# Layer 0 in passes of one head and 1024 rows, with its values and masks brought back from DRAM, in place of layer 1's sums on Pool and the tensor engine

## The chip, the cores and the metric

The kernel runs on one core of one Trainium2 chip. The metric is the device time of one launch in microseconds, the median of the runs shown. Engines are named as the profile names them: PE is the tensor engine (PEld its weight loads), DVE is Vector, ACT is Scalar, POOL is Pool (GpSimd), and SP is the queue that issues most DMAs.

## The reference, cut to what matters

There are N = 4096 nodes with 512 features. The adjacency matrix `adj` holds zeros and ones, with about one in 128 set. Two layers follow each other.

```python
# layer 0: 4 heads of 128; the logit is a sum of a row term and a column term
support = (x @ weight) per head
logits  = f1[None, :] + f2[:, None];   w = where(logits >= 0, logits, 0.2 * logits)
attn    = softmax(w where adj, else -1e30) * mask
x       = layernorm(x + attn @ support + bias + x @ proj_w + proj_b)
# layer 1: 8 heads of 64; queries, keys and values from x
scores  = q @ k.T * 64 ** -0.5 + 0.01 * eye - 1e16 * (1 - max(adj, eye))
x       = layernorm(x + sum over heads of softmax(scores) @ v @ Wo)
```

Because each logit of layer 0 is a sum of two terms, the kernel doesn't exponentiate a 4096 x 4096 matrix there: the weight is a product of factors per row and per column, and a maximum of two such products. In layer 1 the weights are `exp(q.k)` times the transposed mask, and the division by the sum of weights comes after the product with the values.

## The kernel before, in words

The work is written out by hand in program order (`manual_schedule`). Each engine runs its instructions in that order and waits on semaphores; tile pools with a fixed number of buffers (`bufs`) decide when a tile may be written again. The stages follow one another:

1. **Layer 0, prologue.** For each of eight groups of 512 rows (`g`), PE turns x (L616) and multiplies by `weight` (L628, `s_ps`) and `proj_w` (L632, `b_ps`). Vector makes the row and column terms (L639, L642). Pool adds the biases to x (L622) and scales the values (L594). The values of all heads, with a column of ones times the factor, stay in SBUF in one tile, `sup`. PE also turns the adjacency rows of group 0 (`transpose_adj`, L545), four 128 x 128 blocks per column tile, from four row tiles `arow` of 128 x 4096 that Pool's queue loads (L535).
2. **Layer 0, attention.** The loop runs over `g`, over pairs of heads `b` (two) and over 32 column tiles `j`: 512 steps. Of each step, `front` runs three steps ahead of the products. Scalar makes a step function `z` for each of two heads (L682), Vector takes its minimum with the mask (`az`, L685, 1024 wide) and then makes the weights `p`, one instruction of 512 for each of the two heads (L690). PE multiplies: eight products of a 128 x 128 block of `p` with 129 columns of `sup` (L753). They accumulate in four PSUM banks of two heads each, from six buffers. At the last `j`, `finish` takes the denominators (L703, L705) and divides on Scalar (L707) at once. After the second pair of heads, `close` adds `base` on Pool (L714), normalises on Vector (L504 to L515) and stores, and `turn` transposes for layer 1. While the second pair of heads of a group runs, PE turns the adjacency rows of the next group, in every step.
3. **Layer 1, projections.** Keys, queries and values are made (L794, L801, L810) and stored in DRAM.
4. **Layer 1, attention.** There are 32 pairs (`g`, `m`) of 512 queries and two heads, and 32 units `j` in each. A step takes a batch of three units. PE makes the scores (L883) of the batch, two heads side by side, into PSUM tiles `s_ps` of which there are three. Scalar exponentiates in place (L892). Vector multiplies by the mask into SBUF (`p1`, L898), and frees the PSUM tile. PE then does the products with the values (L918) of the batch before.

The sums of weights in layer 1 go two ways. Of 32 units, 22 are added on Pool (L906, L908, in `q_sum`), and ten (`by_tensor`) are summed on PE with a column of ones (L929). The eleventh batch of a pair has only two units. Its third PSUM tile is used to add up the sums of the pair before (L937, L940) and to project one finished row tile (L967):

```python
            def by_tensor(j):
                return j % 6 in (2, 3) and j < NT - 2
...
                chores.append(extent)
                chores.extend(lambda k=k: invert(k) for k in range(8))
```

`divide` copies the sums on Scalar, and hangs the rest into a list, `chores`: two reductions for the check of the range, eight reciprocals of 64 columns each (L957), and later the layernorm of a row tile, whose last step is on Scalar (L981). One chore is done after each mask product, so that no long piece of work stands in Vector's way.

Of the kernel before, what the change touches and what calls it, by code (L numbers as in the profile page):

```python
# [12 lines left out]
ALU = mybir.AluOpType  # L13
# [416 lines left out]
def tile_gat_then_masked_attention(  # L430
# [27 lines left out]
    QD = P // 4  # L458
    CH = 8
    NCH = NT // CH  # L460

# [16 lines left out]
    least = const.tile([P, NG * NP1], F32, name="least")  # L478
    total = const.tile([P, NG * NP1], F32, name="total")
    pick = const.tile([P, HP, KD], F32, name="pick")  # L480
    nc.gpsimd.memset(pick, 0.0)
    for e in range(HP):
        for n in range(2):
            r = (n * HP + e) * QD
            nc.gpsimd.memset(pick[r:r + 1, e, :], 1.0)
# [3 lines left out]
    fr_d = [dram.tile([2, H0, G], F32, name=f"fr_d{g}") for g in range(NG)]  # L489
    adjT_d = [dram.tile([P, NT, G], BF16, name=f"adjT_d{g}") for g in range(NG)]  # L490
# [11 lines left out]
    def moments(y):  # L502
        st = small.tile([P, 6], F32, name="bn_st")
        nc.vector.bn_stats(st, y)  # L504
        mv = small.tile([P, 2], F32, name="bn_mv")
        nc.vector.bn_aggr(mv, st)
        ve = small.tile([P, 1], F32, name="bn_ve")
        nc.gpsimd.tensor_scalar(ve, mv[:, 1:2], EPS, None, op0=ALU.add)
        rs = small.tile([P, 1], F32, name="bn_rs")
        nc.gpsimd.tensor_tensor(rs, ve, minus_half, op=ALU.pow)  # L510
        return mv, rs

    def layernorm(dst, y):
        mv, rs = moments(y)
        nc.vector.tensor_scalar(dst, y, mv[:, 0:1], rs, op0=ALU.subtract, op1=ALU.mult)  # L515
# [3 lines left out]
    W0 = D0 + 1  # L519
    with tc.tile_pool(name="l0", bufs=1) as l0, \  # L520
            tc.tile_pool(name="l0a", bufs=GT) as arow_p, \
            tc.tile_pool(name="l0t", bufs=NCH + 1) as adjT_p:
        sup = l0.tile([P, NT, H0, W0], F32, name="sup")
# [4 lines left out]
        arow = {}  # L528
        adjT = {}

        def load_rows(g):
            arow[g] = []
            for t in range(GT):
                a = arow_p.tile([P, N], BF16, name="arow")
                nc.gpsimd.dma_start(a, adj[(g * GT + t) * P:(g * GT + t + 1) * P, :])  # L535
                arow[g].append(a)

        def transpose_adj(g, j, ps):


            if j % CH == 0:
                adjT[g, j // CH] = adjT_p.tile([P, CH, G], BF16, name="adjT")
            p = ps.tile([P, GT, P], BF16, name="at_ps", bufs=1)
            for t in range(GT):
                nc.tensor.transpose(p[:, t, :], arow[g][t][:, j * P:(j + 1) * P], ident_b)  # L545

            def go():
                dst = adjT[g, j // CH]
                nc.scalar.activation(dst[:, j % CH, :], p.rearrange("p t r -> p (t r)"), AF.Copy)  # L549
                if j % CH == CH - 1:  # L550
                    nc.sync.dma_start(adjT_d[g][:, j - CH + 1:j + 1, :], dst)
                if j == NT - 1:
                    del arow[g]
            return go

        with tc.tile_pool(name="l0s", bufs=2) as sp, \
# [19 lines left out]
            load_rows(0)  # L576
            nc.vector.tensor_add(bb[:, 0, :], bb[:, 0, :], bb[:, 1, :])

            def factors(g):
# [12 lines left out]
                for t in range(GT):  # L592
                    i = t0 + t
                    nc.gpsimd.tensor_tensor(sup[:, i, :, 0:D0], sup[:, i, :, 0:D0],  # L594
                                            a[:, t, :, None].to_broadcast([P, H0, D0]),
                                            op=ALU.mult)
                    nc.gpsimd.tensor_copy(sup[:, i, :, D0], a[:, t, :])

                def rest():
# [3 lines left out]
                    nc.vector.tensor_copy(row, p)  # L603
                    nc.sync.dma_start(
                        fr_d[g].rearrange("k h (t r) -> (k h t) r", r=P), row)
                later.at(3, rest)

            for g in range(NG):
# [12 lines left out]
                for t in range(GT):  # L621
                    nc.gpsimd.tensor_tensor(xg[:, t, :], xg[:, t, :], bb[:, 0, :], op=ALU.add)  # L622
                for t in range(GT):
# [11 lines left out]
                    nc.scalar.activation(sup[:, i, :, 0:D0],  # L635
                                         s_ps.rearrange("p (h d) -> p h d", h=H0), AF.Copy)
                    for k, f in ((0, f1[:, i, :]), (1, f2[:, i, :])):
                        prod = sp.tile([P, H0, D0], F32, name="prod", bufs=1)
                        nc.vector.tensor_tensor(prod, sup[:, i, :, 0:D0],  # L639
# [7 lines left out]
                factors(g)  # L647
# [8 lines left out]
        with tc.tile_pool(name="l0w", bufs=2) as wp, \  # L656
# [3 lines left out]
            HG = 2  # L660
            fr_t, bases, aggs, o_t, p_t = {}, {}, {}, {}, {}

            def load_fr(g, b):
                fr_t[g, b] = wp.tile([P, 2, HG, G], F32, name="fr_t")
                src = fr_d[g]
                nc.sync.dma_start(
                    fr_t[g, b].rearrange("p k h r -> p k (h r)"),
                    bass.AP(tensor=src.tensor, offset=src.offset + b * HG * G,
                            ap=[[0, P], [H0 * G, 2], [1, HG * G]]))

            def front(g, b, j):
                if g == 0 and b == 0 and j == 0:
                    load_fr(g, b)
                if j == 4:
                    if b + 1 < H0 // HG:
                        load_fr(g, b + 1)
                    elif g + 1 < NG:
                        load_fr(g + 1, 0)
                fr = fr_t[g, b]
                z = wp.tile([P, HG, G], BF16, name="z")  # L680
                for e in range(HG):
                    nc.scalar.activation(z[:, e, :], fr[:, 0, e, :], AF.Abs,  # L682
                                         bias=f1s[:, j, b * HG + e:b * HG + e + 1], scale=BIG)
                az = wp.tile([P, HG, G], BF16, name="az")
                nc.vector.tensor_tensor(  # L685
                    az, adjT[g, j // CH][:, j % CH, None, :].to_broadcast([P, HG, G]), z,
                    op=ALU.min)
                p = wp.tile([P, HG, G], F32, name="p", bufs=LA + 1)
                for e in range(HG):
                    nc.vector.scalar_tensor_tensor(  # L690
                        p[:, e, :], fr[:, 1, e, :], dj[:, j, b * HG + e:b * HG + e + 1],
                        az[:, e, :], op0=ALU.max, op1=ALU.mult)
                p_t[g, b, j] = p
                if j == NT - 1:
                    del fr_t[g, b]

            def finish(g, b, o):
                for t in range(GT):
                    i = g * GT + t
                    if b == 0:  # L700
                        aggs[i] = wp.tile([P, H0, D0], F32, name="agg", bufs=GT + 1)
                    den = small.tile([P, HG], F32, name="den")
                    nc.vector.tensor_scalar(den, o[t][:, :, D0], 1e-30, None, op0=ALU.max)  # L703
                    rinv = small.tile([P, HG], F32, name="rinv")
                    nc.vector.reciprocal(rinv, den)  # L705
                    for e in range(HG):
                        nc.scalar.activation(aggs[i][:, b * HG + e, :], o[t][:, e, 0:D0], AF.Copy,  # L707
                                             scale=rinv[:, e:e + 1])
                    if b == H0 // HG - 1:
                        later.at(2 + t, lambda i=i, t=t: close(i, t, g))  # L710

            def close(i, t, g):
                y = aggs.pop(i).rearrange("p h d -> p (h d)")
# [3 lines left out]
                later.at(3, lambda: turn(y, t, g))  # L717

            def turn(y, t, g):
# [3 lines left out]
                later.at(1, lambda: turned(p, t, g))  # L723

            def turned(p, t, g):
                x1T = wp.tile([P, KC, P], F32, name="x1T")
                nc.scalar.activation(x1T, p, AF.Copy)
                nc.sync.dma_start(x1T_d[g][:, :, t * P:(t + 1) * P], x1T)

            steps = [(g, b, j) for g in range(NG) for b in range(H0 // HG) for j in range(NT)]  # L730
            for n in range(LA):
                front(*steps[n])
            for n, (g, b, j) in enumerate(steps):
                if n + LA < len(steps):
                    front(*steps[n + LA])
                if j == 0:
                    o_t[g, b] = [ps.tile([P, HG, W0], F32, name="o_ps", bufs=6)
                                 for _ in range(GT)]
                    if b == 0 and g + 1 < NG:
                        load_rows(g + 1)  # L740
                if j == NT // 2 and b == H0 // HG - 1:
                    for t in range(GT):
                        i = g * GT + t
                        bases[i] = wp.tile([P, D], F32, name="base1", bufs=GT + 1)
                        nc.sync.dma_start(bases[i], base_d[i])
                take = None
                if b == H0 // HG - 1 and g + 1 < NG:
                    take = transpose_adj(g + 1, j, ps)
                o = o_t[g, b]
                p = p_t.pop((g, b, j))  # L750
                for e in range(HG):
                    for t in range(GT):
# [334 lines left out]
```

## Time and profile before

| What | us |
|---|---|
| time, median of 3 runs | 4323.43 (4320.09 to 4325.5) |
| the profiled execution: its time | 4323.43 |
| the profiled execution: span | 4321.6 |
| start to the first product of layer 0 (L753) | 305.6 |
| layer-0 attention, to the last L753 | 305.6 to 1536.1 |
| tail, to the first projection of layer 1 (L794) | to 1568.4 |
| projections, to the first scores (L883) | to 1910.7 |
| layer-1 attention, to the last product (L918) | 1910.7 to 4280.8 |
| end | to 4321.6 |

The engines' busy times over the span: PE 3973.1, DVE 2670.6, ACT 1983.9, POOL 1833.1 us. A busy time is a union: two matmuls that run side by side in different rows or columns of the array count once, so count times mean duration is more than the busy time. Every float32 matmul shows as two instructions. DMA moved 371.76 MB, 86 GB/s on average.

In an answer of the timeline, a line gives the start, the time from there to the end of the merged instructions, the engine, the line of the kernel, the operation and the count, and in brackets how long the engine had been idle and what released it.

### The profile page before, as it was taken

To read this page: it belongs to the slowest core of one execution; us is meant where nothing else is said; L and a number is where in the kernel's file an instruction comes from. 1 tells how busy PE (TensorE), PEld (TensorE's weight loads), DVE (VectorE), ACT (ScalarE), POOL (GpSimd) and SP (SyncE) were. 2 spreads that over 40 slices of the span, in tenths; PEclk is the share of its full clock that TensorE was granted. 3 is DMA by queue.
4 is the path that set the end of the run, shared out by engine and by line. 5 is a ranking of instruction groups with operands and counts; after the bars stand their busy time and mean duration, and the time that the engine had idled before them with its cause. 6 is when DMAs were issued, how large, how long until landed. Compare 5 with 4: busy or idle time off the path is not lost.

```text
span 4321.6 us, 53623 instructions
## 1 busy us (share of the span) xinstructions
PE 3973.1 (92%) x20746; PEld 2040.6 (47%) x20746; DVE 2670.6 (62%) x3488; ACT 1983.9 (46%) x2721; POOL 1833.1 (42%) x1083
## 2 busy tenths in 40 slices
PE   6989889889888879989999999999999999999997
PEld 3448789788888844433323323233222323233232
DVE  3559889888888930125665555655555565555554
ACT  1227677667667610024444444444444444444443
POOL 2220000000000010027777667676767667676765
PEclk8999999999999989999999999999999999999999
DMA  4231341342232032332222222222222223222211
GB/s 136 74 113 45 93 118 50 91 116 73 75 108 74 26 117 97 107 142 75 103 75 71 105 76 78 95 78 76 98 71 100 84 67 111 67 80 93 78 61 43
DMA packets 143674, 371.76 MB, mean 86 GB/s; under 512 B 20016, under 2 KB 53040, under 8 KB 129072
## 3 DMA queue, kind: packets, MB, share of 16 engines
q1 hardware_dynamic: 126848, 318.94, 21.3%
q0 software_dynamic: 6080, 42.99, 4.5%
q10 hardware_dynamic: 10480, 6.29, 0.5%
q8 instruction: 165, 2.70, 0.3%
q14 instruction: 101, 0.83, 0.1%
HBM read 305.14 MB, written 92.41 MB: 92 GB/s over the span
## 4 chain that ended last, share of the span: by engine, by line
PE 51%; DVE 7%; POOL 3%; ACT 2%; DMA 2%; issue 1%; SPq 0%; DVEq 0%; POOLq 0%; ACTq 0%
PE s_ps L883 18%; PE o_ps L918 18%; DVE p L898 4%; PE sm_ps L929 4%; PE k_ps L794 3%; PE v_ps L810 3%; PE q_ps L801 3%; PE s_ps L967 2%; ACT s_ps L892 2%; POOL q_sum L908 2%; DVE p L690 1%; DMA md<-adjT_d 1%; PE s_ps L937 1%; ACT y L981 1%; DVE bn_st L504 0%
## 5 line engine op out<-in xcount | busy, mean ns | idle before, releaser
L908 POOL TENSOR_TENSOR q_sum<-q_sum,p 128x1024 f32<-128x1024 f32 x640 | 1506.7, 2354 | 436.0 <-DVE p L898 398.4
L898 DVE TENSOR_TENSOR p<-s_ps,adjT 128x1024 f32<-128x1024 f32 x896 | 1053.0, 1209 | 737.5 <-ACT s_ps L892 723.8
L892 ACT ACTIVATE s_ps<-s_ps 128x1024 f32<-128x1024 f32 x1024 | 981.1, 1008 | 982.1 <-PE s_ps L883 972.2
L753 PE MATMUL o_ps<-sup,p 128*128 128x129 f32 x8192 | 1055.8, 287 | 92.2 <-DVE rinv L705 54.0
L883 PE MATMUL s_ps<-q_sb,k_sb 64*128 64x512 f32 x4096 | 1034.3, 629 | 103.2 <-DVE p L898 90.0
L753 PEld LDWEIGHTS o_ps<-sup,p 128*128 128x128 f32 x8192 | 995.9, 200 | 119.7 <-ACT agg L707 68.5
L918 PE MATMUL o_ps<-p,v_sb 128*64 128x512 f32 x4096 | 973.3, 610 | 0.0
L682 ACT ACTIVATE z<-fr_t,f1s 128x512 bf16<-128x512 f32 x1024 | 680.4, 718 | 285.9 <-DVE az L685 271.2
L690 DVE SCALAR_TENSOR_TENSOR p<-fr_t,dj,az 128x512 f32<-128x512 f32 x1024 | 724.0, 748 | 54.3 <-PE o_ps L753 1.1
L883 PEld LDWEIGHTS s_ps<-q_sb,k_sb 64*128 64x128 f32 x4096 | 362.7, 189 | 754.7 <-DVE p L898 359.0
L918 PEld LDWEIGHTS o_ps<-p,v_sb 128*64 128x64 f32 x4096 | 267.5, 139 | 681.6 <-issue 652.0
L685 DVE TENSOR_TENSOR az<-adjT,z 128x1024 bf16<-128x1024 bf16 x512 | 350.6, 685 | 54.6 <-ACT z L682 54.6
L535 POOL DMA_DIRECT2D arow<-in_adj_dram x32 | 18.0, 578 | 789.1 <-PE at_ps L545 789.0
L549 ACT ACTIVATE adjT<-at_ps 128x512 bf16<-128x512 bf16 x256 | 153.0, 598 | 147.2 <-PE at_ps L545 146.1
L898 DVE TENSOR_TENSOR p<-s_ps,md 128x1024 f32<-128x1024 f32 x128 | 151.6, 1210 | 105.1 <-ACT s_ps L892 96.8
L906 POOL TENSOR_TENSOR q_sum<-p,p 128x1024 f32<-128x1024 f32 x32 | 75.1, 2345 | 255.0 <-DVE p L898 255.0
L929 PE MATMUL sm_ps<-p,ones 128*32 128x512 f32 x1280 | 170.5, 605 | 0.0
L714 POOL TENSOR_TENSOR agg<-agg,base 128x512 f32<-128x512 f32 x32 | 40.4, 1261 | 279.9 <-ACT agg L707 277.1
L838 POOL DMA_DIRECT2D md<-adjT_d x8 | 5.0, 625 | 352.6 <-DMA v_d<-vg 352.6
L797 DVE COPY kg<-k_ps 128x512 f32<-128x512 f32 x32 | 22.1, 691 | 191.4 <-PE k_ps L794 185.2
L957 DVE RECIPROCAL r<-den 128x64 f32<-128x64 f32 x256 | 136.9, 539 | 0.0
L794 PE MATMUL k_ps<-xT,wk 128*128 128x512 f32 x256 | 117.5, 602 | 11.2 <-DMA xT<-x1T_d 11.2
(89 smaller groups left out, 1972.6 us busy)
## 6 DMA issues: line engine op xcount, KB each, us to landing
k_sb<-k_d SPq DMA_DIRECT2D x128, 512.0 KB, 3.5
v_sb<-v_d SPq DMA_DIRECT2D x128, 512.0 KB, 3.5
arow<-in_adj_dram POOLq DMA_DIRECT2D x32, 1024.0 KB, 18.7
adjT_d<-adjT SPq DMA_DIRECT2D x32, 1024.0 KB, 4.1
adjT<-adjT_d SPq DMA_DIRECT2D x32, 1024.0 KB, 5.7
fr_t<-fr_d SPq DMA_DIRECT2D x16, 1024.0 KB, 8.3
x_sb<-in_x_dram SPq DMA_DIRECT2D x8, 1024.0 KB, 5.6
base_d<-base SPq DMA_DIRECT2D x32, 256.0 KB, 2.0
```

What stands on the lines that cost most here:

```text
L549: nc.scalar.activation(dst[:, j % CH, :], p.rearrange("p t r -> p (t r)"), AF.Copy)
L682: nc.scalar.activation(z[:, e, :], fr[:, 0, e, :], AF.Abs, bias=f1s[:, j, b * HG + e:b * HG + e + 1], scale=BIG)
L685: nc.vector.tensor_tensor(az, adjT[g, j // CH][:, j % CH, None, :].to_broadcast([P, HG, G]), z, op=ALU.min)
L690: nc.vector.scalar_tensor_tensor(p[:, e, :], fr[:, 1, e, :], dj[:, j, b * HG + e:b * HG + e + 1], az[:, e, :], op0=ALU.max, op1=ALU.mult)
L753: nc.tensor.matmul(o[t][:, e, :], p[:, e, t * P:(t + 1) * P], sup[:, j, b * HG + e, :], start=(j == 0 and e == 0), stop=(j == NT - 1), ski ...
L794: nc.tensor.matmul(k_ps, w3["wk"][:, c, m * P:(m + 1) * P], xT[:, c, :], start=(c == 0), stop=(c == KC - 1))
L883: nc.tensor.matmul(s[:, e, :], k[r, a:a + P], qt[g, m][r, :], start=True, stop=True)
L892: nc.scalar.activation(s, s, AF.Exp)
L898: nc.vector.tensor_tensor(p, s, mask.to_broadcast([P, HP, G]), op=ALU.mult)
L908: nc.gpsimd.tensor_tensor(q_sum[g, m], q_sum[g, m], p, op=ALU.add)
L918: nc.tensor.matmul(o[r, :], v[:, j % CH, r], p[:, e, :], start=(j == 0), stop=(j == NT - 1))
L929: nc.tensor.matmul(sm_t[g, m][r:r + QD, :], ones[:, 0:QD], pt[g, m, j - 1 + n][:, e, :], start=(j == 3), stop=(j + 6 >= NT - 2))
```

## The change

It has two parts that share no code. **In layer 0** a pass is one head and 1024 rows (`W`), 16 passes of 32 steps as before. One instruction of 1024 makes `z`, and one makes `p`. `sup` is no longer kept: the prologue writes it to DRAM by head (`sup_d`), and each pass loads its head (`sup_t`, 2.1 MB). The transposed masks are no longer kept either: PE turns eight blocks at a time, Scalar copies them into a small `stage`, and they go to DRAM and come back one pass ahead (`load_adjT0`). Adjacency rows come in pieces of 1024 x 512 with two buffers. The prologue turns 1024 rows in place of 512; in the attention a turn comes every third step of the first 96 of 128 steps. The eight row tiles of a pass take three PSUM banks of six, so a new pass has three free banks; the divisions are spread over the eight steps after the pass, and the closes over every second step.

**In layer 1** the sums on PE, `pick`, `chores` and the batch of two units go. Of 32 units, every third is added on Vector (`qs_d`, in SBUF) and the others on Pool (`qs_p`). Six units after the end of a pair, an item "sum" takes one of the three places of a batch: Vector adds both sums, PE adds over partitions, and Vector does a reciprocal of 512, the product, and two instructions for the check of the range. Two items "y" per group each project two row tiles (in one PSUM tile) and normalise them, on Vector alone but for two small Pool instructions.

```diff
+    W = 1024
@@ layer 0, prologue
+                for h in range(H0):
+                    nc.sync.dma_start(sup_d[h][:, t0:t1, :], sup[:, :, h, :])
+                    if i % CJ == CJ - 1:
+                        load_adjT0(0, i // CJ)
@@ layer 0, front
-                for e in range(HG):
-                    nc.vector.scalar_tensor_tensor(
-                        p[:, e, :], fr[:, 1, e, :], dj[:, j, b * HG + e:b * HG + e + 1],
-                        az[:, e, :], op0=ALU.max, op1=ALU.mult)
+                if j == 2 * LA and n + 1 < len(passes):
+                    load_pass(*passes[n + 1])
+                if h == H0 - 1 and w + 1 < NW and j % CJ == 2:
+                    load_adjT0(w + 1, j // CJ)
+                nc.vector.scalar_tensor_tensor(p, fr[:, 1, :], dj[:, j, h:h + 1], az,
+                                               op0=ALU.max, op1=ALU.mult)
@@ layer 0, end of a pass
+                for t in range(WT):
+                    later.at(1 + t, lambda t=t: divide(t))
+                if h == H0 - 1:
+                    for t in range(WT):
+                        later.at(1 + t, lambda t=t: load_base(w, t))
+                        later.at(4 + 2 * t, lambda t=t: close(w, t))
@@ layer 0, steps
-                if b == H0 // HG - 1 and g + 1 < NG:
-                    take = transpose_adj(g + 1, j, ps)
+                if w + 1 < NW and u % 3 == 0 and u // 3 < NT:
+                    take = transpose_adj(w + 1, u // 3, ps)
@@ layer 1, weigh
-                if by_tensor(j) or j == 0:
-                    return
+                if j % 3 == 2:
+                    if j == 2:
+                        qs_d[g, m] = wp.tile([P, HP, G], F32, name="qs_d")
+                        nc.vector.tensor_copy(qs_d[g, m], p)
+                    else:
+                        nc.vector.tensor_tensor(qs_d[g, m], qs_d[g, m], p, op=ALU.add)
@@ layer 1, the sum of a pair
+            def sum_rows(g, m):
+                q = qs_p.pop((g, m))
+                nc.vector.tensor_tensor(q, q, qs_d.pop((g, m)), op=ALU.add)
...
             def divide(g, m, s):
+                nc.vector.reciprocal(r, s[:, 0, :])
+                nc.vector.tensor_tensor(on_t[g][:, m, :], o_t.pop((g, m)), r, op=ALU.mult)
+                nc.vector.scalar_tensor_tensor(fine, s[:, 0, :], SUM_MIN, fine, op0=ALU.is_ge,
+                                               op1=ALU.mult)
+                nc.vector.scalar_tensor_tensor(fine, s[:, 0, :], SUM_MAX, fine, op0=ALU.is_le,
+                                               op1=ALU.mult)
@@ layer 1, batches
+            for batch in batches:
+                got = [fronts[it[0]](*it[1:]) for it in batch]
+                for it, s in zip(batch, got):
+                    mids[it[0]](*it[1:], s)
+                for it in last:
+                    if it[0] == "unit":
+                        products(*it[1:])
```

In the last fence `fronts` of an item are its scores (`scores`, `sum_rows`, `project`) and `mids` what follows on the other engines (`weigh`, `divide`, `close1`).

## The prediction

> **What bounds the kernel now.** I read the page's engine totals first, then the busy time by stage, then the timeline of one quiet stretch in each attention.
>
> ```profile
> PE 3973.1 (92%) x20746; PEld 2040.6 (47%) x20746; DVE 2670.6 (62%) x3488; ACT 1983.9 (46%) x2721; POOL 1833.1 (42%) x1083
> ```
> ```profile
> 305.00:1536.00 1231.00, 1089.90 (x9199) 1053.06 (x9200) 1103.56 (x1741) 831.73 (x1393) 70.22 (x108) 0.94 0.27 79
> ...
> 2300.00:2700.00 400.00, 384.71 (x1670) 120.07 (x1668) 230.90 (x241) 177.03 (x192) 280.01 (x140) 0.98 0.24 83
> ```
>
> The columns are the stretch, its length, then PE, PEld, DVE, ACT, POOL busy. PE's 92% is two different things. In layer 0 PE and Vector are equally full; in layer 1 PE has 96% and Vector 58%.
>
> ```profile
> 402.46 1.86 PEld L753 LDWEIGHTS o_ps<-sup,p 128*128 128x128 f32 x16
> ...
> 403.26 0.68 DVE L685 TENSOR_TENSOR az<-adjT,z 128x1024 bf16<-128x1024 bf16 x1
> 404.05 1.41 DVE L690 SCALAR_TENSOR_TENSOR p<-fr_t,dj,az 128x512 f32<-128x512 f32 x2
> 404.25 0.32 PEld L545 LDWEIGHTS <-arow 128*128 128x128 bf16 x4
> ...
> 404.52 1.86 PEld L753 LDWEIGHTS o_ps<-sup,p 128*128 128x128 f32 x16
> ```
>
> In layer 0 Vector repeats every 2.12 us (the next `az` is at 405.38). PE's 16 loads take 1.86, with four turns 2.07. So **Vector sets the pace of a step**. The timeline of the pass ends (L703) gives passes of 71.2 us and, where four closes follow, 83.1: a close costs 3.0. Check: 512 x 2.12 = 1085, 28 closes = 84, 16 pass ends at (71.2 - 32 x 2.12) = 3.4 make 54; sum 1223 against 1230 measured. The 3.4 are this:
>
> ```profile
> 378.34 2.17 ACT L707 ACTIVATE agg<-o_ps,rinv 128x128 f32<-128x128 f32 x8 [4.74 <-DVE den L703]
> ...
> 379.01 2.74 PEld L753 LDWEIGHTS o_ps<-sup,p 128*128 128x128 f32 x12 [5.37 <-ACT agg L707]
> ```
>
> A new pass needs four PSUM banks and two are free, so PE waits for the divisions, and Scalar's divisions hold up the next `z`.
>
> ```profile
> 2681.93 2.79 PE L918 MATMUL o_ps<-p,v_sb 128*64 128x512 f32 x12
> ...
> 2684.66 1.07 PE L929 MATMUL sm_ps<-p,ones 128*32 128x512 f32 x8
> ...
> 2685.65 2.85 PE L883 MATMUL s_ps<-q_sb,k_sb 64*128 64x512 f32 x12
> ...
> 2687.94 3.49 DVE L898 TENSOR_TENSOR p<-s_ps,adjT 128x1024 f32<-128x1024 f32 x3 [3.08 <-ACT s_ps L892]
> ...
> 2690.44 9.65 POOL L908 TENSOR_TENSOR q_sum<-q_sum,p 128x1024 f32<-128x1024 f32 x4 [2.36 <-DVE p L898]
> ```
>
> In layer 1 **PE sets the pace**: a batch of three units takes 5.51 us, 6.49 with sums on PE. Vector needs 1.16 for a mask product, Pool 2.41 for an add. A pair takes 74 us.
>
> **What the Trainium skill says.** "SBUF — State Buffer", section "Who interferes with whom": a Vector instruction with two SBUF inputs (or in a two-port mode) and a Pool instruction that reads SBUF exclude each other for a whole instruction. L898 reads PSUM and one SBUF operand, so before it doesn't meet this; the new add of `qs_d` does. The trace agrees in the prologue: `prod` takes 0.69 us alone, and
>
> ```profile
> 72.08 5.38 POOL L622 TENSOR_TENSOR x_sb<-x_sb,bb 128x512 f32<-128x512 f32 x4
> ...
> 75.44 0.89 DVE L639 TENSOR_TENSOR prod<-sup,uv 128x512 f32<-128x512 f32 x1 [3.65 <-ACT sup L635]
> ```
>
> 0.89 beside Pool, whose longest L622 is 1.72 in place of 1.26. L515 has 0.55 alone and 1.48 while L714 runs. Also, Vector gets in between two Pool adds that stand ready. "TensorE: Matmul & The Clock Gate", Part 1: PE falls to half its clock after some idle us. The trace agrees: 16 products take 3.29 us after the wait above, else 2.00.
>
> **Layer 0, part by part.** *Steps.* One `p` instruction of 1024 replaces two of 512. What 512 more elements cost I take from L898 (1209 ns for 1024) and L644 (689 for 512): 0.52. Two starts were 0.705 apart, so a step costs Vector 2.12 - 0.705 + 0.52 = 1.935. Scalar's `z`, by the same kind of slope (L892 1008, L947 597 ns), is 0.72 + 0.41 = 1.13, with a mask copy of 1.0 every third step: 1.5, beside Vector. PE: 1.86, and 0.42 more in every third step that turns eight blocks: 2.00. So PE becomes the bound where it turns, Vector elsewhere.
> Row blocks: w = 0: 96 x 2.00 + 32 x 1.935 = 254. w = 1, 2: 19 steps with eight closes, 19 x 1.935 + 24 = 61, then 77 x 2.00 and 32 x 1.935: 277 each. w = 3: 61 + 109 x 1.935 = 272. Sum 1080. Pass ends: three banks are free, PE waits for nothing; Vector's small ones, 3 x 0.27 a pass, are 13. A slow PE clock after the closes: 10, my choice, 0 to 25. Total 1103 for 1230: **-127**.
> *Prologue.* PE turns 128 blocks more, 32 x 0.26 = +8 (a step is 7.14 us, of which the 16 matmuls are 6.87). The first `bb` landed at 36.3 behind 8 MB of rows; now 2 MB stand before it: of 13 MB 7 are left, 36 x 7/13 = 20: -16. `sup_d` stores wait for Pool in SP's queue, ahead of `base_d` and the next x; x has a group (31 us) of time. The first pass needs its stores landed and 2.1 MB loaded, beside `fr_t` (10.4 us before, when 8 MB of rows shared the queues): +6, bounds 0 and 15. Sum **-2**.
> *Reloads.* 16 `sup_t` and 32 masks add 76 MB to 372; the stage then moves about 190 GB/s, where the first slice of the page shows 136 at 0.4 of the DMA engines. They come a pass ahead: nothing, unless late (below). On Pool's queue a row load waits for PE's turns of the load before last, with the next close's add queued behind it; those turns lie three steps back, and PE is past them. On SP a mask load waits for the mask's last reader with nothing urgent behind it. Layer 1 reads the masks in rows of 1 KB rather than 8, a pair ahead: nothing; `md`, for which Vector waits, 0 to 3 us each, 0 taken.
> *Tail.* Eight closes of 3.3 in place of four, but `x1T` is stored as they go, not after them: **+7**.
>
> **Layer 1, part by part.** *PE's work.* Units stay at 1024 x 1.837 = 1881. Gone: sums 160 x 0.98 = 157; L937 and L940 31 x 1.87 = 58 become 31 x 0.93 = 29; projections stay at 102. PE's work falls from 2198 to 2012, **-186**. Before, 2370 were measured: 172 idle.
> *The new adds.* 9 of 1.2 us a pair (L577, two SBUF inputs, 0.69 for 512; 0.52 for 512 more), a copy (0.6 to 1.2) and the merge 1.2. In a quiet batch Vector has 3 x 1.16 + 1.2 = 4.7 of 5.51; but two Pool adds and one Vector add exclude each other, 4.82 + 1.2 = 6.0. The mask products have 1.6 us before PE needs their PSUM tile (2684.86 for the third, against 2679.15 + 5.51 + 1.85). At 0.5 a batch, with a Pool idle at the start of each stretch, this lasts about 6 of 10 batches: 1 us a pair, **31**.
> *The sum item.* Merge, reciprocal 3.3 (L957: 64 columns 0.43 from start to start), product 0.69, checks 1.4: Vector has 1.2 + 5.4 that stand between mask products, and the item holds one of three PSUM tiles until the checks are done. Worked from the batch start at 0 with the sum in third place: Vector free at 2.8, merge to 4.0, PE's sum waits from 1.85; mask products to 6.35, an add waiting for Pool 7.6, the chain to 13.0; PE, at 9.6, wants that tile for the third scores and waits 3.4. PE loses 2.2 + 3.4 = 5.6; in first place 6.9, in second 6.7. A slow clock adds 1 to 2: 8.3 x 31 = **257**. Bounds: 5 (no lock), 12 (Pool first at every tie).
> *The y items.* Vector waits for two small Pool instructions behind Pool's adds, about 13 us for two tiles; PE's project of 7.3 and scores cover it: 1 x 14. `load_md` (57 us of Vector's idle time before, the wait for `md` and the loads in front) stays, 60.
> Sum: 2012 + 31 + 257 + 14 + 60 = 2374: **+4**. The end, without nine chores in a row: **-3**.
>
> **Total.** -2 - 127 + 7 + 4 - 3 = -121, from 4321.6: 4200.6; 1.8 lie outside the span, and this execution is the median run: **4202**.
>
> **The rivals.**
> *A. The lock costs little.* For: Pool has slack, 52 of 74 us. Against: L639 and L515. The event is 5 and quiet batches 5.51: -31 x 4.3 = -133: 4070.
> *B. Slower: Pool holds the port.* If Pool's waiting add goes first each time, merge and adds each wait 2.4 more: event 12, and quiet batches go at 6.0 rather than 5.51 in 8 of 11, +4 a pair: 31 x (3.7 + 3) = +208: 4410. It decides from a pair of 78 us on: the 121 over 31 is 3.9 a pair. For: a queued Pool add stands ready at nearly each tie. Against: `prod` waited 0.2 us, not a whole add.
> *C. Layer 0 waits for rows.* A 2 MB load has 12 steps, 24 us. Four together now land in a median of 18.7, but in pieces of 16 KB rather than 2. At 30 us it costs 21 x 6 = 126: 4328, no change.
>
> **Numbers.** As worked 0.56 (own range 4120 to 4290), A 0.12, B 0.20, C 0.08, smaller slips 0.04. Under 4090 half of A, above 4400 half of B: 4090 to 4400. A measurement tells 0.2%, 9 us, from no change. Faster 0.70, same 0.06, slower 0.24.
>
> **What would show it.** Layer 0: `p` at 1.27 us, steps of 1.94 and 2.00, no wait of PE on `agg`, 1103 from first to last product. Layer 1: adds on Vector with means over 1.2 and Pool's above 2354 ns; PE idle 5 to 7 us at each sum item, released by Vector's checks; pairs of 74. Wrong, if pairs take over 78, if PE's turns wait for `arow`, or if the layer-0 stage stays above 1200.

## The result and the profile after

The changed kernel takes **4395.13 us** (median of 4 runs, 4381.29 to 4405.39); the kernel before took 4323.35 (4 runs, 4320.09 to 4325.5) beside it. The ratio is **1.0165, 95% interval 1.0136 to 1.0194**: slower by 1.65%, which is clear of the noise, though less than 2%. The forecast was 4202 and faster. The profiled execution is the slowest of the four, 4405.39 with a span of 4403.5, so its stages lie about 10 us above those of the median run in sum.

Stages of both traces, cut at the first and last start of the products that bound them (us):

| | before | after | change | predicted |
|---|---|---|---|---|
| start to first layer-0 product | 305.6 | 314.0 | +8.4 | -2 |
| layer-0 attention, first to last product | 1230.5 | 1178.7 | -51.8 | -127 |
| closes, to the first keys | 32.3 | 41.1 | +8.8 | +7 |
| projections, to the first scores | 342.3 | 342.9 | +0.6 | 0 |
| layer-1 attention, to the last product | 2370.1 | 2490.2 | +120.1 | +4 |
| end | 40.8 | 36.6 | -4.2 | -3 |
| sum | 4321.6 | 4403.5 | +81.9 | -121 |

Two stages are off: layer 0 gained 75 us less than predicted, and layer 1 was put 116 too low. First the engine totals of the page and the stretches that answer to those shown of before (columns: stretch, length, then PE, PEld, DVE, ACT, POOL busy, PE clock, DMA share, GB/s).

```profile
PE 3851.6 (87%) x19338; PEld 1999.3 (45%) x19338; DVE 3364.9 (76%) x3134; ACT 1795.0 (41%) x1953; POOL 2014.4 (46%) x1014
```
```profile
314.00:1493.00 1179.00, 1063.91 (x9048) 1020.52 (x9048) 1032.16 (x1187) 699.83 (x752) 68.62 (x95) 0.97 0.41 120
2300.00:2700.00 400.00, 338.71 (x1330) 105.45 (x1328) 336.31 (x256) 155.99 (x161) 276.43 (x119) 0.94 0.23 75
```

In layer 1 PE fell from 96% to 85%, and Vector rose from 58% to 84%, though PE's work was cut. No engine is full there any more, so what layer 1 lost must be in waits.

**Layer 0**, Vector's timeline around the end of a pass late in the stage, where PE turns nothing:

```profile
1424.10 1.28 DVE L695 SCALAR_TENSOR_TENSOR p<-fr_t,dj,az 128x1024 f32<-128x1024 f32 x1
1425.30 0.68 DVE L693 TENSOR_TENSOR az<-adjT,z 128x1024 bf16<-128x1024 bf16 x1
1426.09 1.28 DVE L695 SCALAR_TENSOR_TENSOR p<-fr_t,dj,az 128x1024 f32<-128x1024 f32 x1
1427.29 0.15 DVE L710 TENSOR_SCALAR den<-o_ps 128x3 f32<-128x3 f32 x1
1427.48 0.18 DVE L713 RECIPROCAL rinv<-den 128x3 f32<-128x3 f32 x1
1429.19 0.69 DVE L693 TENSOR_TENSOR az<-adjT,z 128x1024 bf16<-128x1024 bf16 x1 [1.53 <-ACT z L691]
```

and Scalar's timeline in the same place:

```profile
1422.06 1.15 ACT L691 ACTIVATE z<-fr_t,f1s 128x1024 bf16<-128x1024 f32 x1 [0.84 <-DVE az L693]
1427.75 0.37 ACT L714 ACTIVATE agg<-o_ps,rinv 128x128 f32<-128x128 f32 x1 [4.54 <-DVE rinv L713]
1428.02 1.14 ACT L691 ACTIVATE z<-fr_t,f1s 128x1024 bf16<-128x1024 f32 x1
```

A step is 1.99 us (1424.10 to 1426.09). At the end of a pass, Scalar's next `z` stands behind `agg`, which waits for `rinv`, which stands on Vector behind `p`. Scalar idles 4.54 us. In every step it waits 0.84 for a free `z` buffer; in the other 3.70 it could have made the next `z`. Then Vector idles 1.53 for that `z`. This comes three times a pass, once for each bank.

**Layer 1**: the two groups of adds on the page (busy us, then mean ns).

```profile
L934 POOL TENSOR_TENSOR qs_p<-qs_p,p 128x1024 f32<-128x1024 f32 x672 | 1772.4, 2637 | 566.9 <-DVE p L921 525.7
```
```profile
L928 DVE TENSOR_TENSOR qs_d<-qs_d,p 128x1024 f32<-128x1024 f32 x288 | 589.0, 2045 | 9.9
```

The shortest `qs_d` takes 1.22 us, so 0.82 of each on average is waiting; Pool's mean was 2354 before. A quiet stretch (no y item, no mask load), Vector, then PE; the views end inside the last group of each:

```profile
2604.73 1.29 DVE L928 TENSOR_TENSOR qs_d<-qs_d,p 128x1024 f32<-128x1024 f32 x1
2605.94 2.34 DVE L921 TENSOR_TENSOR p<-s_ps,adjT 128x1024 f32<-128x1024 f32 x2
2609.69 1.22 DVE L921 TENSOR_TENSOR p<-s_ps,adjT 128x1024 f32<-128x1024 f32 x1 [1.41 <-ACT s_ps L915]
2610.95 3.23 DVE L928 TENSOR_TENSOR qs_d<-qs_d,p 128x1024 f32<-128x1024 f32 x1
2614.10 2.34 DVE L921 TENSOR_TENSOR p<-s_ps,adjT 128x1024 f32<-128x1024 f32 x2
```
```profile
2612.90 1.13 PE L910 MATMUL s_ps<-q_sb,k_sb 64*128 64x512 f32 x4
2615.37 1.83 PE L910 MATMUL s_ps<-q_sb,k_sb 64*128 64x512 f32 x6 [1.33 <-DVE p L921]
```

Here the add stands behind the *first* mask product of its batch (1.22, then 3.23, then two products). PE makes one score tile (x4) and waits for the other two, whose buffers the two late products free. The pattern repeats every 12.88 us (PE's wait at 2602.49, 2615.37, 2628.26): 6.44 a batch instead of 5.51. In another group of queries, the same kernel:

```profile
2053.41 3.49 DVE L921 TENSOR_TENSOR p<-s_ps,adjT 128x1024 f32<-128x1024 f32 x3 [0.30 <-ACT s_ps L915]
2056.94 1.91 DVE L928 TENSOR_TENSOR qs_d<-qs_d,p 128x1024 f32<-128x1024 f32 x1
2058.91 3.49 DVE L921 TENSOR_TENSOR p<-s_ps,adjT 128x1024 f32<-128x1024 f32 x3
2062.44 2.14 DVE L928 TENSOR_TENSOR qs_d<-qs_d,p 128x1024 f32<-128x1024 f32 x1
```

The add stands *third*, behind all three products. It waits too, and batches go at 5.5. Units with `j % 3 == 2` don't keep their place: 32 units and a sum item are 33, which keeps it within a group of queries, and the two y items shift it by one from group to group. From first write to first write of `qs_d`, a pair without y items takes 68.6 us where the add is third (groups 0, 3, 6; mean of 10), 74.1 where it is second (groups 1, 4, 7; 8 pairs), 74.1 where it is first (groups 2, 5; 6 pairs). The sum item moves along: it is third, second and first in the same groups. The seven pairs with the y items, six of which also load the next mask, take 98.2.

### The profile page after: what moved, and what is told of

It is laid out like the page before. It is cut to its first block, busy times and chain, and to the rows that moved or that the text cites. A ratio compares the mean times of both kernels' runs of the same rounds, so it can differ in the third digit from the quotient of the medians.

```text
span 4403.5 us, 49845 instructions
## 1 busy us (share of the span) xinstructions
PE 3851.6 (87%) x19338; PEld 1999.3 (45%) x19338; DVE 3364.9 (76%) x3134; ACT 1795.0 (41%) x1953; POOL 2014.4 (46%) x1014
## 4 chain that ended last, share of the span: by engine, by line
PE 41%; DVE 15%; issue 5%; POOL 3%; ACT 2%; DMA 2%; DVEq 0%; SPq 0%; ACTq 0%; POOLq 0%
PE s_ps L910 15%; PE o_ps L944 14%; DVE p L921 8%; DVE qs_d L928 3%; POOL qs_p L934 3%; PE s_ps L973 3%; PE k_ps L804 3%; PE v_ps L820 2%; PE q_ps L811 2%; ACT s_ps L915 2%; DVE qs_p L949 2%; PE s_ps L953 1%; DMA md<-adjT_d 1%; PE o_ps L763 1%; DVE bn_st L505 0%
## 5 line engine op out<-in xcount | busy, mean ns | idle before, releaser
L934 POOL TENSOR_TENSOR qs_p<-qs_p,p 128x1024 f32<-128x1024 f32 x672 | 1772.4, 2637 | 566.9 <-DVE p L921 525.7
L910 PE MATMUL s_ps<-q_sb,k_sb 64*128 64x512 f32 x4096 | 1073.2, 644 | 218.6 <-DVE p L921 162.6
L763 PE MATMUL o_ps<-sup_t,p 128*128 128x129 f32 x8192 | 1020.7, 284 | 107.0 <-DVE p L695 77.3
L763 PEld LDWEIGHTS o_ps<-sup_t,p 128*128 128x128 f32 x8192 | 970.4, 196 | 145.3 <-DVE p L695 89.4
L691 ACT ACTIVATE z<-fr_t,f1s 128x1024 bf16<-128x1024 f32 x512 | 585.0, 1148 | 293.5 <-DVE az L693 266.9
L695 DVE SCALAR_TENSOR_TENSOR p<-fr_t,dj,az 128x1024 f32<-128x1024 f32 x512 | 657.6, 1284 | 54.8 <-DVE az L693 1.8
L928 DVE TENSOR_TENSOR qs_d<-qs_d,p 128x1024 f32<-128x1024 f32 x288 | 589.0, 2045 | 9.9
L549 ACT ACTIVATE stage<-at_ps 128x1024 bf16<-128x1024 bf16 x128 | 129.7, 1013 | 113.3 <-PE at_ps L542 110.0
L953 PE MATMUL s_ps<-qs_p,ones 128*64 128x512 f32 x128 | 55.5, 953 | 109.9 <-DVE qs_p L949 109.9
L645 DVE TENSOR_TENSOR prod<-sup,uv 128x512 f32<-128x512 f32 x64 | 51.3, 801 | 118.5 <-ACT sup L641 118.5
## 6 DMA issues: line engine op xcount, KB each, us to landing
arow<-in_adj_dram POOLq DMA_DIRECT2D x32, 1024.0 KB, 11.1
```

The source lines that it names most:

```text
L691: nc.scalar.activation(z, fr[:, 0, :], AF.Abs, bias=f1s[:, j, h:h + 1], scale=BIG)
L695: nc.vector.scalar_tensor_tensor(p, fr[:, 1, :], dj[:, j, h:h + 1], az, op0=ALU.max, op1=ALU.mult)
L763: nc.tensor.matmul(o[t // BK][:, t % BK, :], p[:, t * P:(t + 1) * P], sup_t[w, h][:, j, :], start=(j == 0 and t % BK == 0), stop=(j == NT ...
L910: nc.tensor.matmul(s[:, e, :], k[r, a:a + P], qt[g, m][r, :], start=True, stop=True)
L928: nc.vector.tensor_tensor(qs_d[g, m], qs_d[g, m], p, op=ALU.add)
L934: nc.gpsimd.tensor_tensor(qs_p[g, m], qs_p[g, m], p, op=ALU.add)
```

## The experiments

Ratios are to the kernel before, run beside them, at 4322.0 to 4323.2 us.

**e1_order.** Is the lost layer-0 gain the order on Scalar's queue?

```diff
-                    later.at(1 + t, lambda t=t: divide(t))
+                    if t % BK == 0:
+                        later.at(1 + t, lambda t=t: invert(t // BK))
+                    later.at(2 + t, lambda t=t: divide(t))
```

(`invert` is the part on Vector, `divide` what is left on Scalar.)

> Layer 0: Scalar's divisions are issued one step after Vector's reciprocals instead of in the same step; nothing else moves. Theory (order of the queues): at each of the 48 bank closes of layer 0 the division stands in Scalar's queue ahead of the next z and waits for a reciprocal that stands in Vector's queue behind p, so Vector waits about 1.55 us for z. With the edit z goes first and the waits vanish: layer-0 attention from 1179 to 1105 us, whole 4395 - 75 = 4320. Rival (Scalar or PE is simply short of time when a pass ends, or rows and banks are late): the waits stay, 1165 to 1179, whole 4380 to 4395.

4316.7 us, ratio 0.9985 (0.9965 to 1.0004): 78 less than the changed kernel. Layer-0 attention goes from 1178.7 to 1111.8, which is 67. The other 11 can't be told from noise: layer 1, whose code is the same, took 2470.4 in this trace and 2490.2 in the other, and executions of the changed kernel alone lie between 4381 and 4405. Vector's timeline:

```profile
1364.67 0.15 DVE L708 TENSOR_SCALAR den<-o_ps 128x3 f32<-128x3 f32 x1
1364.86 0.18 DVE L711 RECIPROCAL rinv<-den 128x3 f32<-128x3 f32 x1
1364.95 0.66 DVE L693 TENSOR_TENSOR az<-adjT,z 128x1024 bf16<-128x1024 bf16 x1
```

`az` follows at once; two ends of banks lie 6.23 us apart in place of 7.87. The order was the cause.

**e2_third and e2_first.** Does the place of the add decide, or does an add cost the same wherever it stands, because Pool holds the shared SBUF port?

```diff
-                if j % 3 == 2:
-                    if j == 2:
+                if n == 2:                  # e2_first: n == 0; n is the place in the batch
+                    if (g, m) not in qs_d:
```

> Layer 1: Vector's share of the sums is taken from the unit that stands third in its batch, in place of the unit with j % 3 == 2, whose place in the batch moves with the sum and y items. Theory (place): a Vector add behind the third mask product delays nobody, one in front of a mask product delays PE's score tiles. Pairs go at 69 us in all groups, the layer-1 stage from 2490 to about 2380, whole 4395 - 110 = 4285. Rival (Pool holds the shared port at every tie, rival B of the prediction): the place doesn't matter, the count of adds is about the same, whole 4375 to 4415.

> The opposite of the run above: Vector's share is always the unit that stands first in its batch. Theory (place): all pairs go as in the groups that have it in first place now, 72 to 75.7 us; the nine pairs that take 69 lose about 5 each, whole 4395 + 45 = 4440 (4410 to 4460). Rival (Pool holds the port wherever the add stands): 4375 to 4415.

Third: 4270.0 us, 0.9875 (0.9859 to 0.9892); a quiet pair takes 67.8 on average of 24. First: 4465.0, 1.0323 (1.0306 to 1.034); 74.9. Now compare the adds themselves, the group of e2_third and then that of e2_first:

```profile
L928 DVE TENSOR_TENSOR qs_d<-qs_d,p 128x1024 f32<-128x1024 f32 x308 | 627.6, 2038 | 10.6
```
```profile
L928 DVE TENSOR_TENSOR qs_d<-qs_d,p 128x1024 f32<-128x1024 f32 x311 | 647.3, 2081 | 10.7
```

Nearly the same number of adds, waiting 0.8 to 0.9 us each, and the two kernels are 195 us apart. **Not how long the add waits, but who stands behind it on its queue.** In third place, three products and an add take 5.73 us (in e2_third 2507.27 to 2513.01), so Vector is still a little over PE's 5.51.

**e3_one_input.** Is it the exclusion, or would 1.2 us of Vector in that place cost as much? The add becomes a reduction of the same tile with one input; this kernel leaves the weights of those units out of the sums.

```diff
-                        nc.vector.tensor_tensor(qs_d[g, m], qs_d[g, m], p, op=ALU.add)
+                        nc.vector.tensor_reduce(one, p.rearrange("p e r -> p (e r)"), AX.X, ALU.add)
```

> Each Vector add of layer 1 is replaced, in its old place, by a reduction of the same tile with one SBUF input and 1024 elements, about as long; the weights of those units (j % 3 == 2 but j = 2) are left out of the sums. The merge and everything else stay. Theory (the add costs because it and Pool's adds exclude each other): the reductions take 1.0 to 1.3 us without waiting, Pool's adds fall back to 2.36 us but for the merge, batches go at 5.51 wherever the unit stands, pairs at 67 to 69, whole 4395 - 110 = 4285. Rival (Vector's time in front of the mask products is enough by itself, lock or no lock): batches stay at 6.4 in the groups with the unit first or second, whole 4375 to 4400.

4229.0 us, 0.9782 (0.9766 to 0.9799); a quiet pair takes 66.7 on average, 66.2 to 67.0 by the place. The reductions (min, median, max ns):

```profile
L929 DVE TENSOR_REDUCE one<-p x288: 1219/1220/1222, 1888.9 to 4188.5; 128x1 f32<-128x1024 f32 x144
```

As long as an add alone, in the old places, and not one waited; Pool's mean fell to 2389 ns. So the loss needs both: the exclusion, and a bad place (66.7 without the one, 67.8 without the other, 74.9 with both in e2_first). The Trainium skill, "SBUF — State Buffer", section "Who interferes with whom", says that a Vector reduction on this chip never meets Pool at the shared ports, and an add of two SBUF inputs does; both groups agree.

**e4_l1_before, e5_order_l1_before.** Do the stages add up? Layer 0 of the changed kernel, or that of e1_order, with the old layer 1.

```diff
+            def of_group(g, j0, j1):
+                r = g * G % W
+                return adjT_d[g * G // W][:, j0:j1, r:r + G]
-                nc.sync.dma_start(at[g, c], adjT_d[g][:, c * CH:(c + 1) * CH, :])
+                nc.sync.dma_start(at[g, c], of_group(g, c * CH, (c + 1) * CH))
```

> The prologue and layer 0 of the changed kernel with the layer 1 of the kernel before (sums on Pool and PE); masks are read from the new layout. Theory (layer 1's loss comes from Vector's adds and the sum item, and the stages add up): the layer-1 stage is 2370 us as before, the earlier stages keep what the changed kernel gains, 35 us: whole 4323 - 35 = 4288. Rival (the masks' new layout in DRAM, pieces of 1 KB, or the shift of what stands before it, slows layer 1): the stage stays near 2490 and the whole near 4395.

> The run above with Scalar's divisions one step after the reciprocals in layer 0. Theory: the 67 to 78 us of e1_order come again, 4288 - 72 = 4216. Rival (a faster layer 0 only moves a wait to the tail or to layer 1's first loads): 4270 to 4288.

4289.5 us, 0.9926 (0.991 to 0.9943), and 4222.5, 0.9768 (0.9752 to 0.9784). In e4 layer 1 runs from 1872.9 to 4242.5, 2369.6 us in place of 2370.1. The new layout of the masks costs nothing; all of layer 1's loss is in the sums and items.

**e6_pe_merge.** What makes the sum item cost 8 us? This is one in the changed kernel, on Vector and then on PE:

```profile
2657.36 1.65 DVE L928 TENSOR_TENSOR qs_d<-qs_d,p 128x1024 f32<-128x1024 f32 x1
2658.94 3.35 DVE L949 TENSOR_TENSOR qs_p<-qs_p,qs_d 128x1024 f32<-128x1024 f32 x1
2664.45 3.36 DVE L960 RECIPROCAL r<-s_ps 128x512 f32<-128x512 f32 x1 [2.16 <-PE s_ps L953]
```
```profile
2654.33 2.79 PE L944 MATMUL o_ps<-p,v_sb 128*64 128x512 f32 x12
2662.44 1.97 PE L953 MATMUL s_ps<-qs_p,ones 128*64 128x512 f32 x4 [5.31 <-DVE qs_p L949]
2664.34 3.79 PE L910 MATMUL s_ps<-q_sb,k_sb 64*128 64x512 f32 x8
```

The merge takes 3.35 instead of 1.21, since it meets an add of the next pair on Pool. PE waits 5.31, and then goes at about half clock: 1.97 and 3.79 for what takes 1.08 and 1.99 in e6_pe_merge. Together 8.0. This item stands first in its batch. PE's wait for the merge is 5.3 there on average, 3.5 where the item is second and 2.1 where it is third. The Trainium skill, "TensorE: Matmul & The Clock Gate", Part 1, says that idle time halves PE's clock; this agrees here (1.97 to 1.08, 3.79 to 1.99).

```diff
-                nc.vector.tensor_tensor(q, q, qs_d.pop((g, m)), op=ALU.add)
+                for n, q in enumerate((qs_d.pop((g, m)), qs_p.pop((g, m)))):
...
+                                         start=(n == 0), stop=(n == 1))
```

> e2_third with the merge of the two sums left to PE: four products into the same PSUM rows in place of Vector's add and two products (four of 0.23 us more for each pair). Theory (at each sum item PE waits for the merge, which waits for a Pool add of the next pair, and PE's clock is low afterwards): PE's wait of 5 us and most of the slow 3 us go, a pair from 67.5 to about 63, whole 4270 - 31 x 4.5 = 4130. Rival (the chain of reciprocal, product and checks on Vector sets the item, as the prediction worked it): PE waits a little later instead, only the merge's own 1.2 us go, 4230 to 4240.

4178.4 us, 0.967 (0.9654 to 0.9686): 92 below e2_third, between the two theories. A quiet pair falls from 67.8 to 65.0. The wait for the merge is gone, and a shorter one comes later, on PE:

```profile
2598.04 2.80 PE L944 MATMUL o_ps<-p,v_sb 128*64 128x512 f32 x12
2603.21 4.55 PE L910 MATMUL s_ps<-q_sb,k_sb 64*128 64x512 f32 x12 [2.38 <-issue]
```

The profile names no releaser for it, but Vector's chain from the reciprocal to the second check runs from 2597.72 to 2603.11 there, and PE goes on as it ends. So both were in the item: the merge ahead, Vector's chain behind. With the merge goes a difference between groups. In e2_third, where the add is third everywhere, a pair still takes 65.7, 68.0 and 71.0 us with the sum item third, second and first; here it takes 65.3, 64.1 and 65.9.

**e7_all, e8_max_last, e9_diag_pool.** e6 with the order of e1; and `load_md` no longer makes Vector stand at the landing (in e2_third `md` was waited for 8.60 us at 2538.88, PE 9.11). Where the diagonal is set differs:

```diff
+                if m == 2 and j == 0 and g + 1 < NG:      # a pair after the load
+                    diagonal(g + 1)                       # e7: four maxima in a row on Vector
# e8: one maximum on Vector at the end of each of four batches
# e9: on Pool, for each tile
+                        nc.gpsimd.tensor_tensor(d, d, off_diag, op=ALU.mult)
+                        nc.gpsimd.tensor_tensor(d, d, ident_e, op=ALU.add)
```

> e6_pe_merge with the layer-0 order of e1_order, and with the four diagonal maxima of a group's mask issued one pair after its load, so that Vector doesn't stand at the load's landing. Theory: 67 to 78 us from layer 0 and 7 x 8.6 = 60 from the mask, whole 4130 - 72 - 60 = 4000. Rival (PE takes the wait elsewhere, its score tiles or Pool's adds being late next): 4060 to 4130.

4072.2 us, 0.9422 (0.9406 to 0.9438): 106 below e6 where 132 was expected, and in the range of the rival. In the traces layer 0 gives 65, as hoped, and layer 1 38 of the 60: the pair that loads the mask is 8 us shorter, but the next loses about 4. The maxima in e7_all:

```profile
2226.83 3.04 DVE L870 TENSOR_TENSOR md<-md,ident_e 128x128 f32<-128x128 f32 x4
```

Four of 0.28, and one wait of 2.2 for Pool ahead of three mask products.

> e7_all with the four diagonal maxima of a group's mask issued one in each of four batches, behind the batch's mask products, in place of four in a row ahead of them. Theory: in e7_all the first maximum (two SBUF inputs) waits 2.4 us for a Pool add, and the mask products and the pair behind it lose 4.4 us, 7 times; behind the mask products that is hidden: 4072 - 7 x 4 = 4044. Rival (those pairs lose for another reason, the mask's load or Vector being full): 4065 to 4075.

4084.4, 0.9447 (0.9431 to 0.9463): **12 slower than e7_all, against both expectations.** The two intervals just overlap, but the runs don't, and the traces have the difference in layer-1 attention (2226.3 and 2239.3). In e8_max_last:

```profile
2233.59 1.12 DVE L871 TENSOR_TENSOR md<-md,ident_e 128x128 f32<-128x128 f32 x1
...
2239.37 2.43 DVE L871 TENSOR_TENSOR md<-md,ident_e 128x128 f32<-128x128 f32 x1
2250.56 0.28 DVE L871 TENSOR_TENSOR md<-md,ident_e 128x128 f32<-128x128 f32 x1
2255.69 2.44 DVE L871 TENSOR_TENSOR md<-md,ident_e 128x128 f32<-128x128 f32 x1
```

Alone, each maximum may meet a fresh Pool instruction. Spread out, one to three of four wait where always one did, and the 28 maxima take 33.3 us instead of 23.0, in batches where Vector has no slack (5.73 against 5.51) or beside the sum item. "Last in the batch is hidden" holds only while there is slack.

> e7_all with the diagonal of a group's mask set by Pool instead of Vector: for each of four tiles one product and one sum of 128 columns on Pool's queue, one pair after the load. Theory (what e7_all and e8_max_last lose is Vector's maxima waiting for Pool adds, once in the former, up to three times in the latter): Pool's own instructions exclude nobody for long and Pool has slack, the pair behind the load goes like the others, 4072 - 7 x 4 = 4044. Rival (Pool's queue is now late for the sum item, or that pair loses for another reason): 4065 to 4090.

4055.2, 0.938 (0.9365 to 0.9396): 17 below e7_all, 11 short of what was expected. Pool's instructions take 0.46 us each. It is the fastest kernel here, 6.2% below the kernel before; what is left of those pairs wasn't followed further.

## Why the prediction was wrong

**Prologue and first loads (-2, measured +8.4).** The first product of the projection came 13.2 earlier (predicted 16). PE's additional turns cost 7.1 (8). The gap to the first layer-0 product grew from 21.3 to 35.8, 14.5 where I had 6, at the edge of its bounds of 0 to 15: the first `fr_t` is issued at 302.69, 17 us after the last stores of `sup_d` begin (285.94), one of which landed at 301.36. Right in kind and undersized; that the stores are what it waits for wasn't tried.

**Layer-0 steps (Vector 1.935, PE 2.00; measured 1.99).** The term that was mis-sized is what 512 more elements of `p` cost, 0.52 by the slope of other operations. Before, 0.625 us passed from the second `p` of 512 to the next `az` (2.12 - 0.79 - 0.705); now 1.20 pass from a `p` of 1024, so it is 0.575. In the sum it cost only 11, as PE was put at 2.00 for most steps.

**Pass ends (0.27 three times a pass; measured 1.90).** This is the step that failed in layer 0. I said "PE waits for nothing" and counted only Vector's small instructions. PE indeed waits for no bank, but it waits for `p` (77.3 us of the stage). I didn't follow Scalar's queue: the division in front of `z` waits for Vector, and Vector then waits for `z`. 1.63 x 45 = 73; e1_order took 67 out of the stage. The change took one wait away at the end of a pass (3.4) and put three in its place (5.7). Closes (3.1 each) were as predicted; the 10 for a cold clock weren't needed. Check: 512 x 1.99 + 24 x 3.1 + 15 x 5.7 = 1179.

**Rival C (rows late)** fell: a row load landed in 11.1 us against the 24 that it has, and PE's turns waited for none.

**Sum item (8.3).** 8.0 in the item shown, which stands first, where I had 6.9 and 1 to 2 for the clock. In the other places it wasn't added up; PE's wait is shorter there. And I named the wrong releaser for most of it. I expected PE's idle time to end with Vector's checks; it ends with the merge all 32 times (109.9 us in sum). The chain behind the merge shows only when the merge is gone (e6).

**Quiet batches (+1 a pair).** This is the step that failed in layer 1. I worked the sum item in all three places, but the add only behind all three mask products. For that place the pair came out right, 58.8 + 0.9 + 1 + 8.3 = 69.0, measured 68.6, with some luck: with the add third throughout, e2_third takes 65.7 there. But five groups of eight have it elsewhere, at 74.1: 14 pairs x 5.5 = 77. The seven pairs with y items and mask took 98.2 where my terms (69.0, and 14 + 60 + 102 over 7) give 94.1: 29. That is 106 of the 116. Not all of it is the add's place: the sum item's place differs in the same groups, and how the 5.5 divides wasn't measured. e2_third moves the adds alone and takes the stage to 2355.7, 115 to 135 less than two traces of the old places (2470.4 and 2490.2). The items' order was in the code; counting 33 items modulo three would have shown it.

**Rival B** named the right direction and nearly the right total (4410; 77.8 us a pair, its limit being 78), by a mechanism that was half wrong, so its close total is in part luck. "Pool's waiting add goes first each time" isn't what happens: at 2604.73 Vector's add gets in after the first of four Pool adds. It waits where it comes just after a Pool add has begun, as at 2610.95; the Trainium skill, "SBUF — State Buffer", section "Who interferes with whom", says "Issue order, not op shape, decides who blocks". And the length of the waiting doesn't decide: e2_third waits as much as e2_first.

**Rival A** (the lock costs little, 4070) fell with e3_one_input, which gains 166 us by taking the adds out of it.

**Tail, projections, `load_md`, end** held within 2 us or weren't changed. The 60 for the mask was 61.4 of Vector's idle time.

## What to carry to other kernels

Follow every engine's queue through an event, not only the one that is the bound: an instruction that waits for another engine holds up all that is issued behind it, so put it one step after what it waits for. An instruction that may wait for a lock belongs behind the work that others wait for, and only if its engine has slack there; write down its place for every iteration, since inserted items shift it. When two kernels have the same busy and waiting times and still differ, look at who stands behind the wait.

## What the runs showed of the hardware

A copy of f32 from SBUF to SBUF on Vector, with one input, waits for Pool too: L926 took 0.75 to 2.76 us in e2_third. The Trainium skill, "SBUF — State Buffer", section "Who interferes with whom", says that a copy can, and I had put it at 0.6 to 1.2. A Pool add that stands ready while Vector has the ports is recorded with the wait in it: 3.22 at 2605.01 in the changed kernel, in place of 2.36.
